# Attention 1, dense blocks: the sources' features as the stationary operand, the clipped counts moving as 256 columns

## The chip, the cores and the metric

The kernel runs on one core of a Trainium2 chip. The metric is the device time of one launch in microseconds (us). Before the change three runs took 5505.89, 5550.96 and 5581.69 us, so the median is 5550.96 us. Engines are named as in the profile: PE (matmuls), PEld (weight loads of PE), DVE (vector), ACT (scalar), POOL (GpSimd) and SP (queue of DMAs). Each has its own list of instructions, whose order is fixed when the program is built, and waits for the others through semaphores.

## The reference

A graph with 6250 nodes and 200000 edges, sorted by destination, passes two layers of attention and then a layer that makes messages from edge attributes. The change touches only the first attention layer (4 heads of 16 features):

```python
feat = (x @ W).reshape(num_nodes, H, D)
el = jnp.sum(feat * attn_l[None], axis=-1)
er = jnp.sum(feat * attn_r[None], axis=-1)
e = jax.nn.leaky_relu(el[src] + er[dst], NEG_SLOPE)
m = jax.ops.segment_max(e, dst, num_segments=num_nodes)
ee = jnp.exp(e - m[dst])
s = jax.ops.segment_sum(ee, dst, num_segments=num_nodes)
alpha = ee / s[dst]
msg = feat[src] * alpha[:, :, None]
rst = jax.ops.segment_sum(msg, dst, num_segments=num_nodes)
return rst + bias.reshape(1, H, D)
```

Each destination node gets a weighted mean of its sources' features, one weight for each edge and head. The weight is exp(leaky_relu(el + er)), which is a product of a source's factor and a destination's factor, and only which of two such products is used depends on the sign of el + er.

## The kernel before

The nodes lie in 49 blocks of 128. In attention 1 the first 31 blocks of destinations ("gather blocks") are computed edge by edge. For each block POOL issues 34 indirect DMAs (L319), each fetching 128 rows of `table1` into a tile `G`, of which there are six buffers of eight fetches. DVE and PE make one-hot matrices and weights (`attend`, L353 to L377: `ohr`, `pe`, `w`, `msg`, `halves`, and the scatter matmul at L377).

The last 18 blocks ("dense blocks", DENSE1 = 18) are computed in 9 pairs by `dense1`, L845 to L940. For these, the kernel first builds a matrix of edge counts for each block of destinations: `count`, L758 to L785, compares indices on DVE (L767), multiplies one-hots on PE (L778), copies on ACT (`ca`, L780) and writes `counts` to DRAM from ACT's queue (L782). A pair then goes over all 49 source blocks in 7 chunks of 7 (HS = 7), and in each chunk over the 4 heads: 9 x 7 x 4 = 252 steps. In one step

- ACT makes a step function `ramp` of el + er, 7 times 128 x 256 (L885),
- DVE takes the minimum of it and of the counts, giving the clipped counts `up`, 128 x 1792 (L887),
- PE adds up (`add`, L891 to L906): for each of the 7 source blocks and each of the 2 destination blocks one weight load of 128 columns of `up` and one matmul in which 102 columns of `rc` move (L905). `rc` holds, for each source, its features times each of the two factors, split into three bf16 parts: 4 heads x 2 factors x 17 x 3 = 408 columns and 2 ones. The result stands with destinations on the partitions, in two PSUM banks `up0` and `up1`, one for each destination block.

Once for each chunk, PE also adds all counts without clipping into `every` (L899): there the features, 103 columns of `rc`, are stationary, and 256 columns of counts move. At the end of a pair (`end`, L910 to L938) ACT copies `every` (L913), PE turns it with 4 transposes (L917), and DVE sums the three parts from the turned tile (L922, twice) and directly from the PSUM of `up0` and `up1` (L926, four times), then subtracts, multiplies by the destination's factors and adds (L929 to L937), and `finish1` makes the rows of the next layer's tables.

`rhs1`, the DRAM copy of `rc`, is filled once by `fill_rhs1` (L682 to L700) in seven pieces during gather blocks 1 and 2.

The three kinds of work are interleaved in the program: after each group of gathers some steps of counting and of `dense1` follow, by due counts. `step` runs a PE part one step after what feeds it. The order within each engine's list is then settled by the framework's scheduler, so lines of neighbouring steps stand mixed there.

The names needed below: `bank()` and `small()` take from one ring of two PSUM banks (`small`), shared by the counting, the transposes and `finish1`. Attention 2 follows after the last end; it doesn't change.

Of the kernel before, what the change touches and what calls it, by code (L numbers as in the profile page):

```python
# [30 lines left out]
F32 = mybir.dt.float32  # L31
# [5 lines left out]
OP = mybir.AluOpType  # L37
AX = mybir.AxisListType
# [4 lines left out]
P = 128  # L43
# [8 lines left out]
HS = 7  # L52
# [14 lines left out]
def gnn_kernel(ctx: ExitStack, tc: tile.TileContext, x, src, dst, attr4, attr8,  # L67
               W1, al1, ar1, b1, W2, al2, ar2, b2,
               Wl0, Wl1, Ws0, Ws1, Wm1, Wm2, Wtp, Wf0, Wf1, src_t, dst_t, attr4_t, attr8_t, out):
    nc = tc.nc  # L70
    N, D = x.shape
    E = src.shape[0]
    NB = -(-N // P)
    FULL = N // P
    REST = N - FULL * P
    HD = W1.shape[1]
    H1, DH = al1.shape
# [38 lines left out]
    def bank():  # L116
        return ps_bank.tile([P, 512], F32, tag="small" if ps_bank is ps_sm else "bank", name="bank")
# [5 lines left out]
    ident = const.tile([P, P], F32, name="ident")  # L123
# [35 lines left out]
    fin = one.enter_context(tc.tile_pool(name="fin1", bufs=1))  # L159
# [8 lines left out]
    for name, v in (("di", dst), ("si", src)):  # L168
        t = find.tile([GP, ROWT + WCAP], I32, name=name)
# [505 lines left out]
    NG = NB - DENSE1  # L675
    dn = one.enter_context(tc.tile_pool(name="dn", bufs=2))
    C1 = 3 * (DH + 1)
    W1R = 2 * H1 * C1 + 2
    rhs1 = dram.tile([P, NB, W1R], BF16, name="rhs1")
    deg1 = pool.tile([P, DENSE1], F32, name="deg1")  # L680

    def fill_rhs1(b0, n):  # L682
        t = dn.tile([P, HS, R1], F32, name="t1c", bufs=1)
        nc.sync.dma_start(t[:, :n], rows_of(table1, b0, n))
        x = dn.tile([P, HS, 2, H1, DH + 1], F32, name="x1", bufs=1)
        for j in range(2):
            ex = t[:, :n, HD + (1 + j) * H1:HD + (2 + j) * H1]
            nc.vector.tensor_tensor(x[:, :n, j, :, :DH], t[:, :n, :HD].rearrange("p b (h d) -> p b h d", h=H1),
                                    ex[:, :, :, None].to_broadcast([P, n, H1, DH]), op=OP.mult)
            nc.vector.tensor_copy(x[:, :n, j, :, DH:], ex[:, :, :, None])  # L690
        r = dn.tile([P, HS, W1R], BF16, name="rc")
        nc.vector.memset(r[:, :, 2 * H1 * C1:], 1.0)
        for j in range(2):
            rj = r[:, :, j * H1 * C1:(j + 1) * H1 * C1].rearrange("p b (f s) -> p b f s", s=3)
            xj = x[:, :n, j].rearrange("p b h d -> p b (h d)")
            nc.scalar.copy(rj[..., 0], xj)
            nc.vector.tensor_tensor(xj, xj, rj[..., 0], op=OP.subtract)
            nc.scalar.copy(rj[..., 1], xj)
            nc.vector.tensor_tensor(rj[..., 2], xj, rj[..., 1], op=OP.subtract)
        nc.sync.dma_start(rhs1[:, b0:b0 + n], r)  # L700

    cut = one.enter_context(tc.tile_pool(name="cut", bufs=1))
# [142 lines left out]
    def dense1():  # L845
# [14 lines left out]
        for b0 in range(NG, NB, 2):  # L860
            n = min(2, NB - b0)
            ahead = load(b0, n, 0)
            erb = dn.tile([P, H1, 2 * P], F32, name="erb", bufs=1)
            for h in range(0, H1, 2):
                pe = bank()
                for j in range(2):
                    for k in range(n):
                        c = j * 2 * P + k * P
                        nc.tensor.matmul(pe[:, c:c + P], er1[:, b0 + k, h + j:h + j + 1].to_broadcast([P, P]), ident,
                                         start=True, stop=True)  # L870
                nc.scalar.copy(erb[:, h:h + 2, :n * P], pe.rearrange("p (j c) -> p j c", j=2)[:, :, :n * P])

            sums = {}
            yield []
            for h0 in range(0, NB, HS):
                ct, r = ahead
                if h0 + HS < NB:
                    ahead = load(b0, n, h0 + HS)
                by_head = r[:, :, :2 * H1 * C1].rearrange("p b (j h f) -> p b j h f", j=2, h=H1)
                for h in range(H1):  # L880
                    ramp = dn.tile([P, HS, 2 * P], BF16, name="ramp1")
                    up = pool.tile([P, LONG], BF16, tag="row", name="up1", bufs=2)[:, :HS * 2 * P].rearrange(
                        "p (h a) -> p h a", h=HS)
                    for i in range(HS):
                        nc.scalar.activation(ramp[:, i, :n * P], erb[:, h, :n * P], AF.Relu,  # L885
                                             bias=sel1[:, h0 + i, h:h + 1], scale=STEEP)
                    nc.vector.tensor_tensor(up[:, :, :n * P].rearrange("p h (a d) -> p h a d", d=QN),  # L887
                                            ramp[:, :, :n * P].rearrange("p h (a d) -> p h a d", d=QN),
                                            ct[:, :n].rearrange("p k a h d -> p h (k a) d"), op=OP.min)

                    def add(h0=h0, h=h, r=r, ct=ct, up=up, by_head=by_head, b0=b0, n=n, sums=sums):  # L891
                        if h0 + h == 0:
                            sums["ups"] = [ps_dn.tile([P, 512], F32, tag=f"up{k}", name=f"up{k}")[:, :2 * H1 * C1].rearrange(
                                "p (h j f) -> p h j f", h=H1, j=2) for k in range(n)]
                            sums["every"] = ps_dn.tile([P, 2, 2 * P], F32, tag="every", name="every")
                        ups, every = sums["ups"], sums["every"]
                        for i in range(HS if h == 0 else 0):
                            for j in range(2):
                                nc.tensor.matmul(every[:HH + 1, j, :n * P].rearrange("p (k d) -> p k d", d=QN),  # L899
                                                 r[:, i, (2 + j) * HH:(3 + j) * HH + 1],  # L900
                                                 ct[:, :n, :, i, :].rearrange("p k a d -> p (k a) d"),
                                                 start=h0 + i + j == 0, stop=h0 + i + j == NB)
                        for i in range(HS):
                            for k in range(n):
                                nc.tensor.matmul(ups[k][:, h], up[:, i, k * P:(k + 1) * P], by_head[:, i, :, h, :],  # L905
                                                 start=h0 + i + h == 0, stop=h0 + i + h == NB + H1 - 2)  # L906

                    yield [add]

            def end(b0=b0, n=n, sums=sums):  # L910
                ups, every = sums["ups"], sums["every"]
                whole = dn.tile([HH + 1, 2, 2 * P], F32, name="whole", bufs=1)
                nc.scalar.copy(whole[:, :, :n * P], every[:HH + 1, :, :n * P])  # L913
                turned = bank().rearrange("p (k j c) -> p k j c", k=2, j=2)
                for k in range(n):
                    for j in range(2):
                        nc.tensor.transpose(turned[:, k, j, :HH + 1], whole[:, j, k * P:(k + 1) * P],  # L917
                                            ident[:HH + 1, :HH + 1])
                s2 = dn.tile([P, 2, H1, DH + 1], F32, name="s2", bufs=1)
                v = dn.tile([P, 2, 2, H1, DH + 1], F32, name="v1", bufs=1)  # L920
                for k in range(n):
                    nc.vector.tensor_reduce(s2[:, k].rearrange("p (j h) d -> p j (h d)", j=2),  # L922
                                            turned[:, k, :, :HH].rearrange("p j (f s) -> p j f s", s=3),
                                            axis=AX.X, op=OP.add)
                    for j in range(2):
                        nc.vector.tensor_reduce(v[:, k, j], ups[k][:, :, j].rearrange("p h (d s) -> p h d s", s=3),  # L926
                                                axis=AX.X, op=OP.add)
                nc.vector.tensor_copy(deg1[:, b0 - NG:b0 - NG + n, None], turned[:, :n, 1, HH:HH + 1])
                nc.vector.tensor_tensor(v[:, :n, 1], s2[:, :n], v[:, :n, 1], op=OP.subtract)  # L929
                for j in range(2):  # L930
                    nc.vector.tensor_tensor(v[:, :n, j], v[:, :n, j],
                                            pq[:, b0:b0 + n, j * H1:(j + 1) * H1, None].to_broadcast([P, n, H1, DH + 1]),
                                            op=OP.mult)
                total = fin.tile([P, 2, HD + H1], F32, name="sumsd")
                nc.vector.tensor_add(total[:, :n, :HD].rearrange("p k (h d) -> p k h d", h=H1), v[:, :n, 0, :, :DH],
                                     v[:, :n, 1, :, :DH])
                nc.vector.tensor_add(total[:, :n, HD:, None], v[:, :n, 0, :, DH:], v[:, :n, 1, :, DH:])  # L937
                finish1(b0, n, total[:, :n, :])  # L938

            yield [end]  # L940
# [549 lines left out]
```

## Time and profile before

| what | value | from |
|---|---|---|
| median of three runs | 5550.96 us | times |
| the profiled execution | 5588.02 us, span 5586.3 us | times, page |
| mean granted clock of PE | 0.720 | page |
| PE, DVE, ACT, POOL busy over the span | 61%, 63%, 52%, 47% | page, part 1 |
| weight loads of L905 | 272.9 us busy, x3528, 131 ns mean | page, part 5 |
| `up` on DVE (L887) | 273.8 us, x252, 1087 ns mean | page, part 5 |
| L905 first and last start | 510.4 and 2403.7 us | rows of this line |

The profiled execution is one launch, 37 us above the median. Steps of `dense1` run from about 500 to 2400 us after the span's start, beside the gathers and the counting; attention 2 lies at about 2420 to 3000 us, the message layer after it. In a line of groups the name of the tile written stands before the arrow, the tiles read after it; then come the number of instructions, the busy time in us, the mean in ns, and behind the second bar the idle time just before them with what ended most of it. A busy time counts overlapped instructions of one engine once, so it is smaller than the number times the mean.

### The profile page before, as it was taken

What the parts mean: (1) busy time and instruction counts of PE and PEld (TensorE: products, weight loads), DVE (VectorE), ACT (ScalarE), POOL (GpSimd) and SP (SyncE); (2) the same over time, 40 slices, a digit from 0 to 9 for tenths busy, and PEclk for the clock granted to TensorE, in tenths of its full rate; (3) what the DMA queues carried; (4) which work ended last, traced back from release to release, by engine and by line L of the source; (5) the groups of instructions that cost most, each with busy time, mean ns of one, the idle gap of its engine ahead of it and who ended that gap; (6) DMA issues with size and microseconds to landing.
All of it is one profiled execution on the core that took longest, in us unless ns stands there. A gap on an engine that the chain in (4) does not pass through costs nothing. (4 is left out here: it accounts for less than half of the span.)

```text
span 5586.3 us, 66809 instructions
## 1 busy us (share of the span) xinstructions
PE 3395.3 (61%) x22075; PEld 2519.0 (45%) x22076; DVE 3498.1 (63%) x5531; ACT 2900.8 (52%) x6921; POOL 2639.6 (47%) x2684
## 2 busy tenths in 40 slices
PE   3124554644555545569995566676667666677676
PEld 2124444544444445558884334344434344444444
DVE  4255555655656655668885566666666666666667
ACT  2024655754655656669995344444444444444444
POOL 2655545545345445310003555555556556555553
PEclk9998555655666556669997676767767666767667
DMA  4243433433334434454442111111111111111111
GB/s 105 60 125 98 120 109 110 137 104 108 110 113 118 118 101 118 115 188 151 163 165 70 45 48 47 46 49 48 48 47 49 46 48 49 48 47 49 47 48 30
DMA packets 348033, 480.97 MB, mean 86 GB/s; under 512 B 190602, under 2 KB 236208, under 8 KB 343695
## 3 DMA queue, kind: packets, MB, share of 16 engines
q1 hardware_dynamic: 199014, 238.86, 14.2%
q0 software_dynamic: 85776, 147.31, 11.2%
q10 hardware_dynamic: 62872, 90.28, 4.6%
q8 instruction: 181, 2.97, 0.2%
q14 instruction: 190, 1.55, 0.1%
HBM read 367.21 MB, written 108.97 MB: 85 GB/s over the span
## 5 line engine op out<-in xcount | busy, mean ns | idle before, releaser
L319 POOL DMA_INDIRECT G<-table,srcc x1563 | 1475.4, 944 | 1556.8 <-issue 676.6
L319 POOL DMA_INDIRECT G<-table,srcw x1054 | 1091.9, 1036 | 987.3 <-DVE w L362 384.4
L1300 PE MATMUL whole<-halves,ohr 128*128 128x512 f32 x1563 | 798.7, 647 | 24.3 <-issue 23.3
L885 ACT ACTIVATE ramp<-erb,sel 128x256 bf16<-128x256 f32 x1764 | 756.5, 499 | 1.9 <-DVE up L887 1.6
L1252 ACT ACTIVATE hid<-big 128x512 f32<-128x512 f32 x392 | 233.9, 597 | 951.5 <-PE big L1250 419.5
L780 ACT CAST ca<-small 128x392 bf16<-128x392 f32 x784 | 350.2, 482 | 644.3 <-remote 413.0
L778 PE MATMUL small<-key,lo 128*128 128x98 bf16 x3136 | 339.0, 260 | 484.3 <-ACT ca L780 213.3
L1300 PEld LDWEIGHTS whole<-halves,ohr 128*128 128x128 f32 x1563 | 418.1, 283 | 438.2 <-issue 373.7
L1250 PE MATMUL big<-a8t,wm_sb 16*128 16x512 f32 x392 | 294.5, 840 | 394.8 <-issue 346.6
L1274 ACT ACTIVATE g<-G,a 128x128 f32<-128x128 f32 x1563 | 506.9, 401 | 11.2 <-DMA G<-table,srcc 9.6
L1181 ACT ACTIVATE ramp<-erb,sel 128x256 bf16<-128x256 f32 (+1 forms) x1225 | 491.8, 499 | 23.5 <-DVE up L1185 16.8
L778 PEld LDWEIGHTS <-lo 128*128 128x128 bf16 x3136 | 262.4, 128 | 533.5 <-issue 523.0
L767 DVE TENSOR_TENSOR lo<-slots,turned 128x2048 bf16<-128x2048 bf16 x196 | 239.5, 1222 | 418.5 <-remote 206.0
L1293 DVE TENSOR_TENSOR halves<-mess,halves 128x1024 fp32r<-128x1024 f32 x196 | 239.1, 1220 | 350.6 <-ACT halves L1287 201.2
L1250 PE MATMUL big<-hid,wm_sb 128*128 128x512 f32 x392 | 356.7, 1011 | 112.4 <-ACT hid L1252 99.0
L905 PE MATMUL up<-rc,up 128*128 128x102 bf16 x3528 | 323.5, 268 | 144.8 <-DVE up L887 106.4
L1258 PE MATMUL big<-wtp_sb,hid 64*128 64x128 f32 x3126 | 289.4, 331 | 142.6 <-issue 79.0
L1258 PEld LDWEIGHTS big<-wtp_sb,hid 64*128 64x128 f32 x3126 | 244.2, 229 | 246.9 <-issue 140.0
L377 PE MATMUL whole<-halves,ohr 128*128 128x136 f32 x1054 | 248.1, 388 | 173.1 <-issue 80.0
L905 PEld LDWEIGHTS <-up 128*128 128x128 bf16 x3528 | 272.9, 131 | 176.5 <-DVE up L887 127.3
L887 DVE TENSOR_TENSOR up<-ramp,ctc 128x1792 bf16<-128x1792 bf16 x252 | 273.8, 1087 | 97.2 <-ACT ramp L885 64.2
L377 PEld LDWEIGHTS whole<-halves,ohr 128*128 128x128 f32 x1054 | 218.3, 294 | 185.2 <-issue 84.5
(294 smaller groups left out, 6252.9 us busy)
## 6 DMA issues: line engine op xcount, KB each, us to landing
counts<-ca ACTq DMA_DIRECT2D x196, 392.0 KB
ct<-counts SPq DMA_DIRECT2D x192, 392.0 KB
rc<-rhs SPq DMA_DIRECT2D x63, 717.5 KB
oht<-dlow SPq DMA_DIRECT2D x31, 1088.0 KB
ctc<-counts SPq DMA_DIRECT2D x504, 56.0 KB
G<-table,srcc POOLq DMA_INDIRECT x1563
G<-table,srcw POOLq DMA_INDIRECT x1054
a8t<-attr_rows SPq DMA_DIRECT2D x391, 16.0 KB
```

Of the source, the lines that this page charges most:

```text
L319: nc.gpsimd.indirect_dma_start(out=G[:, c, :], out_offset=None, in_=table, in_offset=bass.IndirectOffsetOnAxis(ap=idx[:, c:c + 1], axis=0))
L377: nc.tensor.matmul(acc, oh[:, c, :], ms[:, c].rearrange("e s f -> e (s f)"), start=start and c == 0, stop=stop and c == n - 1)
L778: nc.tensor.matmul(ps[:, k * NKEY:(k + 1) * NKEY], lo[:, a, :, r], ky[:, a, :, r], start=True, stop=True)
L780: nc.scalar.copy(ca[:, :, i * W:(i + WBANK) * W].rearrange("p h (k d) -> p h k d", d=W), ps[:, :WBANK * NKEY].rearrange("p (k h d) -> p h ...
L885: nc.scalar.activation(ramp[:, i, :n * P], erb[:, h, :n * P], AF.Relu, bias=sel1[:, h0 + i, h:h + 1], scale=STEEP)
L887: nc.vector.tensor_tensor(up[:, :, :n * P].rearrange("p h (a d) -> p h a d", d=QN), ramp[:, :, :n * P].rearrange("p h (a d) -> p h a d", d ...
L905: nc.tensor.matmul(ups[k][:, h], up[:, i, k * P:(k + 1) * P], by_head[:, i, :, h, :], start=h0 + i + h == 0, stop=h0 + i + h == NB + H1 - 2)
L1181: nc.scalar.activation(ramp[:, h, :n * P], erb[:, :n * P], AF.Relu, bias=sel2[:, h0 + h, :], scale=STEEP)
L1250: nc.tensor.matmul(ph, w, (hid[-1] if j else x)[:, :npr * P], start=True, stop=True)
L1258: nc.tensor.matmul(pw[:, c, :], hid[1][half, j * P:(j + 1) * P], wtp_sb[half].rearrange("x p u -> x (p u)"), start=True, stop=True)
L1274: nc.scalar.activation(g0[:, c], G[:, c, :], AF.Copy, scale=a0[:, c, :])
L1300: nc.tensor.matmul(acc, oh[:, c, :], ms[:, c].rearrange("e s h i u -> e (s h i u)"), start=start, stop=stop)
```

## The change

Stationary and moving operand of the clipped sums change places, as they already stand for `every`. For each source block and head there is now one weight load of 102 columns of `rc` and one matmul in which both blocks' `up`, 256 columns, move. The sums stand with features on the partitions, so the end of a pair copies them from PSUM (`some`, two copies on ACT), turns them with 8 transposes on PE into two more banks of the ring, and sums the parts from there. So that the 102 columns of one head are contiguous, and that `every` still has two runs of 103, `rc` is laid out by pairs of heads (205 columns: 102 of one head, a one, 102 of the next, with the two factors in swapped order), and the operations of `fill_rhs1` and of the end are split by head of the pair.

```diff
-    W1R = 2 * H1 * C1 + 2
+    HW = 4 * C1 + 1
+    W1R = H1 // 2 * HW
...
-        x = dn.tile([P, HS, 2, H1, DH + 1], F32, name="x1", bufs=1)
+        x = dn.tile([P, HS, H1 // 2, 2, 2, DH + 1], F32, name="x1", bufs=1)
         for j in range(2):
-            ex = t[:, :n, HD + (1 + j) * H1:HD + (2 + j) * H1]
-            nc.vector.tensor_tensor(x[:, :n, j, :, :DH], t[:, :n, :HD].rearrange("p b (h d) -> p b h d", h=H1),
-                                    ex[:, :, :, None].to_broadcast([P, n, H1, DH]), op=OP.mult)
-            nc.vector.tensor_copy(x[:, :n, j, :, DH:], ex[:, :, :, None])
+            ex = t[:, :n, HD + (1 + j) * H1:HD + (2 + j) * H1].rearrange("p b (q h) -> p b q h", h=2)
+            for h in range(2):
+                xh = x[:, :n, :, h, j if h == 0 else 1 - j]
+                nc.vector.tensor_tensor(
+                    xh[..., :DH], t[:, :n, :HD].rearrange("p b (q h d) -> p b q h d", h=2, d=DH)[:, :, :, h],
+                    ex[:, :, :, h, None].to_broadcast([P, n, H1 // 2, DH]), op=OP.mult)
+                nc.vector.tensor_copy(xh[..., DH:], ex[:, :, :, h, None])
...
                         if h0 + h == 0:
-                            sums["ups"] = [ps_dn.tile([P, 512], F32, tag=f"up{k}", name=f"up{k}")[:, :2 * H1 * C1].rearrange(
-                                "p (h j f) -> p h j f", h=H1, j=2) for k in range(n)]
+                            sums["ups"] = [ps_dn.tile([P, 2, 2 * P], F32, tag=f"up{k}", name=f"up{k}")
+                                           for k in range(H1 // 2)]
...
+                        q, h = divmod(h, 2)
                         for i in range(HS):
-                            for k in range(n):
-                                nc.tensor.matmul(ups[k][:, h], up[:, i, k * P:(k + 1) * P], by_head[:, i, :, h, :],
-                                                 start=h0 + i + h == 0, stop=h0 + i + h == NB + H1 - 2)
+                            c = q * HW + h * (2 * C1 + 1)
+                            nc.tensor.matmul(ups[q][:2 * C1, h, :n * P], r[:, i, c:c + 2 * C1], up[:, i, :n * P],
+                                             start=h0 + i + h == 0, stop=h0 + i + h == NB)
...
+                some = dn.tile([2 * C1, H1 // 2, 2, 2 * P], F32, name="some", bufs=1)
+                for q in range(H1 // 2):
+                    nc.scalar.copy(some[:, q, :, :n * P], ups[q][:2 * C1, :, :n * P])
...
+                for h in range(2):
+                    c = h * (C1 + 1)
+                    nc.vector.tensor_reduce(s2[:, :n, :, h], turned[:, :n, :, c:c + C1].rearrange(
+                        "p k j (f s) -> p k j f s", s=3), axis=AX.X, op=OP.add)
...
                 for k in range(n):
-                    nc.vector.tensor_reduce(s2[:, k].rearrange("p (j h) d -> p j (h d)", j=2),
-                                            turned[:, k, :, :HH].rearrange("p j (f s) -> p j f s", s=3),
+                    turned = bank().rearrange("p (h c) -> p h c", h=H1)
+                    for h in range(H1):
+                        nc.tensor.transpose(turned[:, h, :2 * C1], some[:, h // 2, h % 2, k * P:(k + 1) * P],
+                                            ident[:2 * C1, :2 * C1])
+                    nc.vector.tensor_reduce(v[:, k].rearrange("p q h j d -> p (q h) (j d)"),
+                                            turned[:, :, :2 * C1].rearrange("p h (f s) -> p h f s", s=3),
                                             axis=AX.X, op=OP.add)
-                    for j in range(2):
-                        nc.vector.tensor_reduce(v[:, k, j], ups[k][:, :, j].rearrange("p h (d s) -> p h d s", s=3),
-                                                axis=AX.X, op=OP.add)
...
-                nc.vector.tensor_tensor(v[:, :n, 1], s2[:, :n], v[:, :n, 1], op=OP.subtract)
-                for j in range(2):
-                    nc.vector.tensor_tensor(v[:, :n, j], v[:, :n, j],
-                                            pq[:, b0:b0 + n, j * H1:(j + 1) * H1, None].to_broadcast([P, n, H1, DH + 1]),
-                                            op=OP.mult)
+                for h in range(2):
+                    vh = [v[:, :n, :, h, j if h == 0 else 1 - j] for j in range(2)]
+                    nc.vector.tensor_tensor(vh[1], s2[:, :n, :, h], vh[1], op=OP.subtract)
                     for j in range(2):
+                        f = pq[:, b0:b0 + n, j * H1:(j + 1) * H1].rearrange("p b (q h) -> p b q h", h=2)[:, :, :, h, None]
+                        nc.vector.tensor_tensor(vh[j], vh[j], f.to_broadcast([P, n, H1 // 2, DH + 1]), op=OP.mult)
...
```

The two additions that make `sumsd` (L935 and L937) are likewise split in two, one for each head of the pair.

## The prediction

> **What bounds the kernel now.** I read the groups of the page first, to see what the touched lines cost, then the engines by stretch, then the list of waits, then the order in time.
>
> ```profile
> L319 POOL DMA_INDIRECT G<-table,srcw x1054 | 1091.9, 1036 | 987.3 <-DVE w L362 384.4
> ...
> L885 ACT ACTIVATE ramp<-erb,sel 128x256 bf16<-128x256 f32 x1764 | 756.5, 499 | 1.9 <-DVE up L887 1.6
> ...
> L905 PE MATMUL up<-rc,up 128*128 128x102 bf16 x3528 | 323.5, 268 | 144.8 <-DVE up L887 106.4
> ```
>
> The line to be changed is the last: 323.5 us of PE, in 252 groups of 14. Before it PE waited 106.4 us for `up` from DVE. In the same steps ACT's ramp takes 756.5 us, so in a dense step alone ACT has 3.0 us, PE 1.28 us and DVE 1.09 us of work.
>
> ```profile
> 560.00:2400.00 1840.00, 995.64 (x9040) 891.18 (x9040) 1081.16 (x1910) 1101.36 (x2699) 863.13 (x825) 0.60 0.40 113
> 2520.00:2940.00 420.00, 384.13 (x4065) 346.92 (x4063) 360.07 (x648) 420.00 (x1077) 0.00 (x0) 1.00 0.47 160
> ```
>
> Columns: stretch, length, busy us of PE, PEld, DVE, ACT, POOL, granted clock, DMA share, GB/s. In the stage of the change (first row) no engine is full: PE 54%, DVE 59%, ACT 60%, POOL 47%. In attention 2 (second row) ACT is full. So the first stage isn't set by an engine but by engines waiting for each other in turn:
>
> ```profile
> POOL G L319 <- DVE w L362: 359.7, 37, 40.4
> ...
> DVE lo L767 <- PE small L778: 165.7, 89, 14.1
> ACT ca L780 <- PE small L778: 143.1, 110, 16.3
> ...
> PE up L905 <- DVE up L887: 104.7, 80, 4.5
> ```
>
> These are totals over the same 1840 us (us, times, longest). POOL's fetches stand still for 547 us in all until DVE gives a buffer of `G` back (359.7 for L362, 117.1 for L367, 71 for smaller lines), and 79.5 us more for a fetch of the next run; with them 627 of 1840 us, 34%. In the rest POOL issues, about 1.25 us for each fetch (945 ns and 0.30 idle), and DVE, ACT and PE stand still when they need a fetch that isn't there. So a delay of DVE counts in full in about a third of the stage, and in the rest is partly covered by fetches that run anyway. I take one half, with a third and all as bounds, for what a delay in the middle of the stage is worth. Nobody waits long for L905 itself: its own releases are 12.4 us (ACT), 6.0 and 1.4 us (DVE). It counts by what stands behind it on PE, L778 above all.
>
> **The clipped sums on PE.** Removed: 3528 loads and 3528 matmuls of 102 columns. Added: 1764 of each, with 256 columns. The new form isn't in the trace, but `every` (L899) is nearly it: 103 stationary columns of `rc`, 256 columns moving, bf16.
>
> ```profile
> 794.55 3.20 PE L899 MATMUL every<-ctc,rc 128*103 128x256 bf16 x14
> ...
> 1555.50 1.37 PE L905 MATMUL up<-rc,up 128*128 128x102 bf16 x14
> ...
> 1578.61 1.69 PE L899 MATMUL every<-ctc,rc 128*103 128x256 bf16 x14
> ...
> 1667.88 0.82 PE L905 MATMUL up<-rc,up 128*128 128x102 bf16 x14
> ```
>
> Rows of PE in order of time: start, length, line, count. Each line has a slow and a fast form. 14 old matmuls take 1.37 or 0.82 us; less one matmul's own length (283 and 206 ns) that is 84 or 47 ns from start to start. 14 of `every` take 3.20 or 1.69 us, less 421 and 270 ns: 213 or 109 ns. One new matmul replaces two old ones: 213 for 168, or 109 for 94. For a step of 7: +0.31 us slow, +0.10 us fast. The mean old group is 323.5/252 = 1.28 us, which is 84% slow and 16% fast, so +0.28 us a step and **+70 us** of PE over 252 steps. Halving the count of instructions gains nothing, because the old ones were already paced by their columns (204 for two) and the new ones are by 256. Bounds: a third to all of it, 23 to 70 us; I take half, **+35 us**.
>
> A weight load of 128 columns of `up` takes 144 ns at the median, one of 103 of `rc` 207 ns; 3528 against 1764 is 508 against 365 us. Both lie under matmuls that are spaced by their columns, so I count no gain; if loads did set the pace it would be -143 us, which only rival C uses. The Trainium skill (TensorE: Matmul & The Clock Gate, section Weight-path perf modes) says that fast weight load works only with 128 weights that aren't fp32, so the 102 columns lose it. That speaks against the change, and by it each load would be up to twice an old one, no gain from half the number; the rows give 1.4 times.
>
> The same page (section What's actually happening) says that PE's clock opens only after about 3.4 us of sustained work. The trace has 0.60 in this stage and 1.00 in attention 2. By that rule groups of 1.70 us for 1.37 us would open it a little more often; I found no way to size it and put nothing in the sum.
>
> **The end of a pair, 9 times.** In the rows of one end the sums stand like this:
>
> ```profile
> 1572.48 1.20 DVE L926 TENSOR_REDUCE v<-up 128x68 f32<-128x204 f32 x4 [1.07 <-remote]
> ...
> 1574.66 0.90 PE L917 MATMUL bank<-ident,whole 103*128 103x103 f32 x4
> ```
>
> DVE reads `up` at once, and only `every` goes over ACT and PE. After the change everything does. ACT: two copies of 102x512, each like L913 (586 ns), +1.2 us. PE: 8 transposes of 102 columns; four of L917 take 0.90 us, so +1.8 us. DVE: four sums at 360 ns go, two of twice that size come; L1198, 390 elements, takes 556 ns, so about 575 ns each: 1.44 against 1.15. Subtract, multiply and add are split by head, 5 operations become 10; the smallest there is 160 ns and the old ones 280 to 290 ns, so some 0.6 us more. DVE together +0.3 us. The copies and transposes are links of one chain, overlapping in part, then a sum: about 2.5 us later for the results at each end, 22 us over 9. DVE's list in the built program has the two new sums directly behind those of `every`, and `msg`, `halves` and the next `w` behind them: whoever waits for these gives `G` back to POOL. PE has the transposes ahead of L377 and `every`, ACT has the second copy, which waits for the last add, ahead of `halves`; and the two extra banks come out of the ring of two that the counting uses. Bounds: 0 (all under gathers) to 5 us an end, 45 us; I take **+22 us**. SP and POOL get no new instruction, and no DMA changes its size.
>
> **fill_rhs1, 7 times.** Each of 14 multiplications (615 ns for 448) becomes two of 224; with 283 ns for 128 each is about 385 ns, +0.15. Each of 14 small copies (182 ns) becomes two, +0.15. Together +4 us on DVE; ACT's casts keep their number and size. Bounds 0 to 8 (strides), I take **+4 us**.
>
> **Sum.** 35 + 22 + 4 = +61 us. On the profiled execution's 5588 us that is 5649; that execution lay 37 us above the median, and the terms are absolute, so from the median it is 5551 + 61 = **5612 us**, +1.1%. Lowest and highest by the bounds: +23 and +123.
>
> **Rivals.** A verdict needs 2%, 111 us, which is also about what a measurement of this kernel can tell from no change (the three runs spread over 76 us).
>
> B, slower by over 2%: the turn at the pair's end becomes a stop of the whole ring. DVE stands at the new sums until ACT has copied and PE has turned; behind it stand the lines that free `G`, POOL stops, and its fetches are then missing. One such stop of POOL lasts 359.7/37 = 9.7 us now. Nine of 10 us are 90 us, with the 39 above 129: 5680 us. If PE's 70 us count in full too: 5715. It decides from 8 us an end ((111 - 39)/9). For: in the row above, waits for PE inside an end are already there, and the longest are 40 us. Against: the sums of `every` already made this detour at the same place, and DVE waited only a few us in all there (2.8 for L360, 0.8 for L917).
>
> C, faster by over 2%: the built program keeps nearly all of the order elsewhere but moves gathers' lines around each end on DVE and PE. If that, or PE's shorter list, takes away a third of POOL's 359.7 us, that is -120; with the loads setting PE's pace (-143, by half -72) in place of +35, and the other 26 kept, -166: 5385 us. The order alone, -120 + 61, gives 5492 and no verdict; between the two the case begins at 5440. For: these waits are of one line, long and few. Against: nothing in the rows shows loads setting the pace, and a moved line can as well make a wait longer.
>
> D, that it doesn't do what it says: the built program has 1764 loads and matmuls for 3528 each, so this is out, except that the moving 256 columns might cost other than `every`'s.
>
> **How the numbers follow.** The forecast, a small loss or nothing that can be told, 0.46. B 0.36: its point is 8 us an end, and small delays in a ring of waiting engines tend to grow. C 0.18. The range goes from the upper part of C, 5440, to B with all of PE, 5720; the forecast's own is 5560 to 5660. Faster 0.18, same 0.46, slower 0.36.
>
> **What would show it.** In the changed profile: matmuls of the clipped sums x1764 with about 213 or 109 ns from start to start and a group of 7 at 1.7 or 0.9 us, PE busy there about 390 us in place of 323.5; loads x1764 at about 200 ns; two copies of about 590 ns and 8 transposes at each end; the stage from 500 to 2400 us longer by some 60 us and attention 2 and the message layer unchanged. POOL's waits for DVE in that stage above 650 us speak for B, below 430 for C. A mean clock far from 0.60 there, or `up` matmuls that start closer than 213 ns at the slow clock, would make the prediction wrong.

## The result, and the profile after

The changed kernel takes 5541.78 us (median of 20 runs, 5523.15 to 5577.78), the kernel before, run beside it, 5548.45 us (20 runs, 5494.07 to 5581.69). The ratio on record, which isn't simply that of the two medians (0.9988), is 1.0003, with a 95% interval of 0.9981 to 1.0025: no difference, where +1.1% was forecast. One plain fact is needed to read what follows: launches of either kernel took about 5550 us in some of the comparisons and about 4431 us in others, alike within one comparison and both on the same chip (two of the chips gave both), so every ratio below is to the kernel before in the same comparison, and "at 5550" or "at 4431" says which kind it was.

The groups of the changed kernel's profile (span 5563.5 us, before 5586.3):

```profile
L319 POOL DMA_INDIRECT G<-table,srcw x1054 | 1084.7, 1029 | 915.1 <-DVE w L362 373.5
...
L892 ACT ACTIVATE ramp<-erb,sel 128x256 bf16<-128x256 f32 x1764 | 756.7, 499 | 4.4 <-DVE up L894 2.1
...
L785 PE MATMUL small<-key,lo 128*128 128x98 bf16 x3136 | 323.2, 253 | 376.3 <-issue 182.1
...
L913 PE MATMUL up<-up,rc 128*102 128x256 bf16 x1764 | 364.8, 371 | 133.2 <-DVE up L894 101.9
...
L913 PEld LDWEIGHTS <-rc 128*102 128x102 bf16 x1764 | 302.4, 179 | 149.4 <-issue 142.3
...
L377 PE MATMUL whole<-halves,ohr 128*128 128x136 f32 x1054 | 234.0, 373 | 158.0 <-DVE halves L332 89.8
```

The count is halved, as the diff says, and PE's own line grew, but from 323.5 to 364.8 us, by 41 and not by 70. The counting's matmuls (L785, before L778), whose code is the same, fell from 339.0 to 323.2 us, and those of L377 from 248.1 to 234.0. So most of the 41 us came back on other lines of PE, whose single matmuls got shorter (L785 253 ns in the mean for 260, L377 373 for 388). The same stretches as before show it too:

```profile
560.00:2400.00 1840.00, 1006.80 (x7397) 913.81 (x7397) 1081.81 (x1932) 1109.99 (x2717) 854.94 (x825) 0.63 0.40 113
2520.00:2940.00 420.00, 384.07 (x4070) 347.03 (x4070) 361.51 (x654) 420.00 (x1077) 0.00 (x0) 1.00 0.48 162
```

In the stage of the change the granted clock is 0.63 for 0.60, and PE's busy time 1006.8 for 995.6 us. The stage itself did not lengthen: `up` matmuls start from 522.9 to 2400.5 us, before from 510.4 to 2403.7. Attention 2 is as it was. The waits of that stretch (total us, times, longest):

```profile
POOL G L319 <- DVE w L362: 349.1, 29, 48.4
...
ACT ca L787 <- remote: 294.6, 57, 32.1
...
DVE lo L774 <- PE small L785: 191.4, 96, 14.0
...
POOL G L319 <- DVE msg L367: 152.3, 17, 42.2
...
DVE lo L774 <- remote: 131.8, 14, 25.8
```

The waits of POOL's fetches of `G` for DVE make 552 us for 547, in the middle between the marks set for B (650) and C (430): neither came. Two rows end in "remote", that is, the profile found no instruction whose end released the engine. They were there before as well, larger than any row that the prediction showed but one, and it read past them:

```profile
ACT ca L780 <- remote: 348.3, 84, 15.4
...
DVE lo L767 <- remote: 196.4, 25, 26.6
```

The parts of the change look as costed. PE in order of time, start, length, count, two groups of 7:

```profile
1407.64 1.70 PE L913 MATMUL up<-up,rc 128*102 128x256 bf16 x7
...
1461.41 0.93 PE L913 MATMUL up<-up,rc 128*102 128x256 bf16 x7
```

1.7 or 0.9 us, the two forms that were read off `every`. And one end of a pair:

```profile
922.91 0.59 ACT L929 COPY some<-up 102x512 f32<-102x512 f32 x1 [1.33 <-PE up L913]
...
924.81 0.89 PE L940 MATMUL bank<-ident,some 102*128 102x102 f32 x4
...
925.73 0.58 DVE L942 TENSOR_REDUCE v<-bank 128x136 f32<-128x408 f32 x1
...
926.28 0.89 PE L940 MATMUL bank<-ident,some 102*128 102x102 f32 x4
...
927.21 0.58 DVE L942 TENSOR_REDUCE v<-bank 128x136 f32<-128x408 f32 x1 [0.63 <-PE bank L940]
```

Copies, transposes and sums have the lengths of the prediction (590, 900 for four, 575 ns), and DVE stands 0.63 us at the second sum here; over all 18 such sums it waits 5.5 us for the transposes.

### The profile page after: what moved, and what is told of

It is laid out like the page before. It is cut to its first block, busy times and chain, and to the rows that moved or that the text cites. A ratio compares the mean times of both kernels' runs of the same rounds, so it can differ in the third digit from the quotient of the medians.

```text
span 5563.5 us, 63519 instructions
## 1 busy us (share of the span) xinstructions
PE 3408.7 (61%) x20383; PEld 2536.5 (46%) x20384; DVE 3504.3 (63%) x5586; ACT 2909.2 (52%) x6939; POOL 2630.0 (47%) x2684
## 3 DMA queue, kind: packets, MB, share of 16 engines
q0 software_dynamic: 85776, 147.31, 11.2%
## 5 line engine op out<-in xcount | busy, mean ns | idle before, releaser
L785 PE MATMUL small<-key,lo 128*128 128x98 bf16 x3136 | 323.2, 253 | 376.3 <-issue 182.1
L1200 ACT ACTIVATE ramp<-erb,sel 128x256 bf16<-128x256 f32 (+1 forms) x1225 | 491.6, 496 | 22.7 <-DVE up L1204 17.8
L785 PEld LDWEIGHTS <-lo 128*128 128x128 bf16 x3136 | 257.5, 124 | 417.0 <-issue 401.7
L913 PE MATMUL up<-up,rc 128*102 128x256 bf16 x1764 | 364.8, 371 | 133.2 <-DVE up L894 101.9
L913 PEld LDWEIGHTS <-rc 128*102 128x102 bf16 x1764 | 302.4, 179 | 149.4 <-issue 142.3
L377 PE MATMUL whole<-halves,ohr 128*128 128x136 f32 x1054 | 234.0, 373 | 158.0 <-DVE halves L332 89.8
L377 PEld LDWEIGHTS whole<-halves,ohr 128*128 128x128 f32 x1054 | 204.5, 278 | 179.0 <-DVE halves L332 94.6
```

The source lines that it names most:

```text
L377: nc.tensor.matmul(acc, oh[:, c, :], ms[:, c].rearrange("e s f -> e (s f)"), start=start and c == 0, stop=stop and c == n - 1)
L785: nc.tensor.matmul(ps[:, k * NKEY:(k + 1) * NKEY], lo[:, a, :, r], ky[:, a, :, r], start=True, stop=True)
L913: nc.tensor.matmul(ups[q][:2 * C1, h, :n * P], r[:, i, c:c + 2 * C1], up[:, i, :n * P], start=h0 + i + h == 0, stop=h0 + i + h == NB)
L1200: nc.scalar.activation(ramp[:, h, :n * P], erb[:, :n * P], AF.Relu, bias=sel2[:, h0 + h, :], scale=STEEP)
```

## The experiments

The expectations name theories by number or letter. Theories 1 and B: PE and the ends have slack, so that next to nothing counts on any launch. Theory 2: PE's time counts by about half, as forecast, and something else gave it back. Theory A: the forecast's cost is real, and at 5550 the waits without a releaser cover it. Theory C, not the rival C of the prediction: the turn is dear, the matmuls are a gain, and the two cancel. Where they speak of a slower and a faster chip, read 5550 and 4431.

### First comparison, at 4431: doses of PE work

A dose is the same work in another amount. **e1_pe_twice** puts a second matmul, with zeros stationary, behind each of the 1764; **e2_pe_3_more** does so for 3 of the 7 source blocks only.

```diff
+                            if i < 7:      # e2: 3
+                                nc.tensor.matmul(ups[q][:2 * C1, h, :n * P], none, up[:, i, :n * P],
+                                                 start=False, stop=h0 + i + h == NB)
```

> The changed kernel with a second matmul behind each of the 1764 of the clipped sums: same 256 columns moving, same PSUM, a stationary tile of zeros, so it adds nothing to the result and about 1764 x 213 ns = 376 us at the slow clock, 192 us at the fast one, to PE. Theory 1 (PE has slack in this stage: the ring of fetches and DVE sets the pace and PE's work lies beside it): less than +40 us on the kernel before. Theory 2 (as in the prediction: PE's time counts by about half, and the change's cost was given back by something else, order or clock): +100 to +190 us.

> The same with the second matmul for only 3 of every 7 source blocks: 756 more matmuls, +82 to +161 us of PE. Theory 1: within 15 us of the kernel before, and less than 3/7 of what the full doubling costs (a threshold). Theory 2: +40 to +80 us, 3/7 of the doubling (proportional).

Measured: 1.0105 (1.0089 to 1.0120), 4478.06 us, and 1.0092 (1.0078 to 1.0106), 4473.22 us, the kernel before taking 4431.27.

**e3_pe_seventh** goes the other way: one source block of each seven is added.

```diff
-                        for i in range(HS):
+                        for i in range(1):
```

> The changed kernel with only the first source block of each chunk of seven added into the clipped sums (left out: six sevenths of these sums, so the attention of the dense blocks is not the reference's). PE loses 1512 of 1764 matmuls and loads, about 310 us of busy time. Theory 1: 0 to -20 us. Theory 2: -100 to -160 us.

Measured: 1.0037 (1.0023 to 1.0051), 4447.08 us.

**e4_end_twice** copies, turns and sums twice at each end.

```diff
-                for q in range(H1 // 2):
+                for q in (*range(H1 // 2), *range(H1 // 2)):
...
-                for k in range(n):
+                for k in (*range(n), *range(n)):
```

> The changed kernel with the new part of each pair's end done twice: the two copies of the sums, the eight transposes and the two sums of parts. Theory 1 (the end's extra time goes under fetches that run anyway): within 15 us of the kernel before. Theory 2 (each end pays what it is delayed by): 9 ends x 2.5 to 5 us = +22 to +45 us. If the ring stops as in the rival that ends slower: +90 us.

Measured: 1.0096 (1.0081 to 1.0112), 4470.52 us.

All four lie above 1. Read against the kernel before, as the expectations do, e1 (+46 us) and e3 (+16 us) fit neither theory, since a part of the loss is in all four. Between themselves they can be read at once: e1 is 0.68% above e3, 30 us, and its PE is busy 228.6 us more (lines below), so 13% of that PE time shows in the time, give or take 4%. What the changed kernel itself does at 4431 came only with h1 below.

### Second and third comparisons, at 5550: each part alone

**a1_after** is the changed kernel again, **b1_before** a single launch of the kernel before. **a3_no_turn** drops the copies, transposes and their banks, and makes the sums from the tile that is there already:

```diff
-                for q in range(H1 // 2):
-                    nc.scalar.copy(some[:, q, :, :n * P], ups[q][:2 * C1, :, :n * P])
...
-                    for h in range(H1):
-                        nc.tensor.transpose(turned[:, h, :2 * C1], some[:, h // 2, h % 2, k * P:(k + 1) * P],
-                                            ident[:2 * C1, :2 * C1])
```

**b2_turn_only** is the kernel before with only the new end: copies of `up0` and `up1`, 8 transposes, two sums for four.

```diff
+                for k in range(n):
+                    nc.scalar.copy(some[:, k, :2 * H1 * C1], ups[k][:2 * C1].rearrange("p h j f -> p (h j f)"))
...
-                    for j in range(2):
-                        nc.vector.tensor_reduce(v[:, k, j], ups[k][:, :, j].rearrange("p h (d s) -> p h d s", s=3),
-                                                axis=AX.X, op=OP.add)
```

> The changed kernel itself, on the chip of this call. Its first comparison was on a chip where the kernel before takes 5548 us; the first experiments ran on one where it takes 4431 us, and there all four variants of the changed kernel were 0.4 to 1.05% above the kernel before. Theory A (the change costs what was worked out, or half of it, and on the first chip the waits with no releaser in the trace cover it): +0.6 to +1.0% where the kernel before takes about 4430 us, 0 where it takes about 5550 us. Theory B (PE and the end have slack on any chip, and the variants' own edits cost what they showed): within 0.3% on either.

> The first part of the change alone: the matmuls with 256 columns moving and the new layout stay, but the end of a pair neither copies the clipped sums nor turns them; DVE sums parts of the turned tile of all counts in their place (left out: the clipped sums never reach the result; the shares' denominators are held above 1 so that numbers stay finite). Theory A with the end as the cost: equal to the kernel before within 0.2%. Theory A with PE's columns as the cost: as the changed kernel, +0.5 to +1.0% on the faster chip. Theory B: within 0.3%.

> The second part alone: the kernel before with its 3528 matmuls of 102 columns, and at each pair's end two copies by ACT, eight transposes by PE and two sums of 408 elements by DVE in place of the four sums from PSUM (left out: the clipped sums are turned as if they stood by features, so the dense blocks' result is not the reference's; denominators held above 1). Theory A with the end as the cost: as the changed kernel, +0.5 to +1.0% on the faster chip. With PE's columns as the cost: within 0.2%. Theory B: within 0.3%.

> The kernel before, for its profile on the chip of this call: theory A expects next to no waits without a releaser in the stage of the dense blocks where the time is about 4430 us, and ACT and DVE busy for about 80% there; theory B says nothing of it.

Measured, the kernel before at 5577.1 us: a1 0.9999 (0.9977 to 1.0022), a3 0.9950 (0.9926 to 0.9975), b2 1.0041 (1.0015 to 1.0068); b1 5559.48 us. That looked like theory C: the matmuls a gain of 0.5%, the turn a loss of 0.4 to 0.5%. So both were run again, beside **f1_turn_later**, where the end is two steps, ACT's copies in the first and the rest in the next:

```diff
+                sums["copied"] = whole, some
+
+            yield [end]
+
+            def turn(b0=b0, n=n, sums=sums):
...
-    n_dense = -(-DENSE1 // 2) * (2 + H1 * (NB // HS))
+    n_dense = -(-DENSE1 // 2) * (3 + H1 * (NB // HS))
```

> The changed kernel again. Theory C, formed on the last call (two effects that cancel: with half as many instructions on PE the clipped sums gain about 0.5%, the end of a pair loses about 0.4%): 1.000 where the kernel before takes about 5550 us. Theory B (slack, the parts' differences were their own order of instructions): the same. On the faster chip, if the gain of the sums comes from PE's late events alone, it is missing there and the loss stays: +0.4 to +0.8%.

> The matmuls with 256 columns and the new layout alone, without copies and turn at the end, as before (the clipped sums never reach the result; denominators held above 1). Theory C: 0.995 again on a chip where the kernel before takes about 5550 us; on the faster chip, where PE's events are not late, 1.000 to 1.004. Theory B: 1.000 within 0.2% on either.

> The kernel before with the copies, transposes and sums of the new end alone, as before (its dense blocks' result is not the reference's; denominators held above 1). Theory C: 1.004 again on the slower chip, and +0.4 to +0.7% on the faster one, since the chain ACT, PE, DVE is there on any chip. Theory B: 1.000 within 0.2%.

> The changed kernel with its end in two steps: the three copies of ACT in one, the transposes, DVE's sums and the rest one step later, so that PE and DVE come to the turned sums when the copies are long done. Theory C: the loss of the end goes and the gain of the sums stays, 0.995 of the kernel before on the slower chip, faster than both. Theory B: as the changed kernel, 1.000.

Measured, the kernel before at 5549.69 us: c1 0.9980 (0.9957 to 1.0003), c3 0.9991 (0.9967 to 1.0016), c2 1.0007 (0.9980 to 1.0033), f1 0.9985 (0.9966 to 1.0003). Neither part repeated. The same pair of kernels moved by 0.3 to 0.4% between two comparisons, more than one interval holds, so parts below about 0.4% cannot be told here, and moving the turn gained nothing over the changed kernel. The traces do part the two where the clock is concerned: in the stretch from 560 to 2400 us it is 0.63 and 0.64 with the new matmuls alone (a3, c3), as in the changed kernel, and 0.61 and 0.60 with the turn alone (b2, c2), as in the kernel before.

### Fourth comparison, at 5550: the doses

The edits of e1 and e4 once more, with the changed kernel beside them.

> The changed kernel, as the base of the two others. Where the kernel before takes about 5550 us: 0.998 to 1.002. Where it takes about 4430 us: theory A (the worked-out cost is real, and only the late waits cover it) 1.005 to 1.010; theory B (slack on any chip) 0.998 to 1.002.

> The changed kernel with a second matmul (stationary zeros, the same 256 columns) behind each of the clipped sums: nine times the PE time that the change added. On the slower chip: theory B and A both within 0.3% of the changed kernel, if the waits cover PE; if PE's time is paid by half and was given back by something else, +2 to +3%. On the faster chip: 1.0105 of the kernel before, as measured; the difference from the changed kernel is then the price of 365 us of PE.

> The changed kernel with the copies, transposes and sums of the new end done twice. On the slower chip: within 0.3% of the changed kernel if ends go under other waits, +0.4% if each end pays about 2.5 us. On the faster chip: 1.0096 of the kernel before, as measured; under theory A the changed kernel is then about half of that above 1, under theory B at 1.000.

Measured, the kernel before at 5569.98 us: g1 0.9995 (0.9973 to 1.0017), g2 1.0077 (1.0053 to 1.0102), g3 1.0021 (0.9997 to 1.0044). The page's groups of g2, and the stage in g1 and then in g2:

```profile
L915 PE MATMUL up<-up,rc 128*102 128x256 bf16 x1764 | 523.4, 325 | 138.3 <-DVE up L896 98.9
...
L918 PE MATMUL up<-up,none 128*102 128x256 bf16 x1764 | 523.6, 326 | 10.3 <-issue 9.6
```

```profile
560.00:2400.00 1840.00, 995.57 (x7394) 902.69 (x7393) 1079.31 (x1930) 1105.37 (x2713) 851.80 (x826) 0.64 0.40 113
560.00:2400.00 1840.00, 1088.63 (x8822) 997.95 (x8821) 1052.85 (x1887) 1061.66 (x2602) 862.39 (x831) 0.74 0.39 111
```

The two lines overlap each other, so together they are busy some 524 us: twice the matmuls for 364.8 us once is +44%, not +100%, with the clock at 0.74. Over the whole span PE's busy time goes from 3394.7 (g1) to 3516.2 us, +121.5. The time goes up by 0.82% of 5570, 46 us: 38% of what PE was really given, give or take 15%. Theories A and B had both expected less than 0.3% here, so both missed.

### Fifth and sixth comparisons, at 4431: the changed kernel, and without its turn

**h1_after** is the changed kernel, **k1_no_turn** the edit of a3, **k2_before** a single launch of the kernel before.

> The changed kernel once more, for the chip it falls on. Where the kernel before takes about 4430 us: 1.005 to 1.010 if the change's cost is real and only the late waits of the slower chip cover it; 0.998 to 1.002 if PE and the ends have slack on any chip. Where it takes about 5550 us: 0.998 to 1.002, as in all comparisons so far.

> The matmuls with 256 columns and the new layout alone, no copies and no turn at the end (the clipped sums never reach the result; denominators held above 1). Where the kernel before takes about 4430 us: 1.000 to 1.002 if the turn is the cost, 1.005 to 1.008 if it is the matmuls, the layout or the order of instructions that they bring. Where it takes about 5550 us: 0.995 to 1.000, as twice before.

> The kernel before, for its profile beside the last run. Where it takes about 4430 us: ACT and DVE busy for about 80% of 500 to 1700 us, next to no waits without a releaser; the stage of the dense blocks ends some 25 to 35 us earlier than in the changed kernel if the cost lies there, and the filling of the operands near 250 to 350 us some 4 us earlier.

Measured: h1 1.0080 (1.0065 to 1.0096), 4464.11 us for 4430.4; k1 1.0030 (1.0017 to 1.0043), 4442.86 us for 4432.59; k2 4435.64 us. So at 4431 there is a loss, about 35 us, in the range that theory A gave, and 22 us of it (uncertain by 9) go with the turn. With h1 the first four can be read; the two comparisons' medians of the kernel before lie within 1 us. The line of engine totals of each page, for k2, h1, e1, e2 and e3:

```profile
PE 3130.2 (71%) x22075; PEld 2356.0 (53%) x22076; DVE 3480.2 (78%) x5531; ACT 2920.3 (66%) x6921; POOL 2668.8 (60%) x2684
```

```profile
PE 3129.0 (70%) x20383; PEld 2369.9 (53%) x20384; DVE 3487.3 (78%) x5586; ACT 2925.9 (66%) x6939; POOL 2665.3 (60%) x2684
```

```profile
PE 3213.2 (72%) x22147; PEld 2468.5 (55%) x22148; DVE 3491.6 (78%) x5587; ACT 2926.3 (65%) x6939; POOL 2655.7 (59%) x2684
```

```profile
PE 3166.5 (71%) x21139; PEld 2403.2 (54%) x21140; DVE 3489.7 (78%) x5587; ACT 2928.3 (65%) x6939; POOL 2663.1 (60%) x2684
```

```profile
PE 2984.6 (67%) x18871; PEld 2192.7 (49%) x18872; DVE 3487.7 (78%) x5586; ACT 2930.5 (66%) x6939; POOL 2658.2 (60%) x2684
```

The change leaves PE's total at 3129.0 for 3130.2 us: nothing was added. The stretch from 500 to 1800 us, for k2, e3, h1, e2 and e1 (the number after the five engines is the granted clock):

```profile
500.00:1800.00 1300.00, 892.40 (x8699) 815.00 (x8699) 1037.76 (x1857) 1044.00 (x2585) 882.84 (x824) 0.66 0.54 155
500.00:1800.00 1300.00, 764.71 (x5700) 663.51 (x5700) 1032.64 (x1870) 1046.36 (x2584) 884.54 (x829) 0.59 0.54 154
500.00:1800.00 1300.00, 887.40 (x7010) 814.01 (x7009) 1024.65 (x1858) 1034.84 (x2557) 891.43 (x830) 0.72 0.54 153
500.00:1800.00 1300.00, 908.36 (x7617) 840.65 (x7617) 1016.91 (x1844) 1025.32 (x2531) 886.69 (x830) 0.79 0.53 152
500.00:1800.00 1300.00, 961.14 (x8463) 897.87 (x8462) 1014.53 (x1836) 1015.90 (x2514) 876.34 (x827) 0.84 0.53 152
```

The doses give one price:

| against h1 | PE busy | time | share | clock, 500 to 1800 us |
|---|---|---|---|---|
| e3, a seventh | -144.4 us | -0.43%, -19 us | 13% | 0.59 |
| h1, the changed kernel | 0 | 0 | | 0.72 |
| e2, 3 of 7 twice | +37.5 us (3166.5) | +0.12%, +5 us | 14% | 0.79 |
| e1, all twice | +84.2 us | +0.25%, +11 us | 13% | 0.84 |

Each difference of two ratios is uncertain by about 0.2%, so the single shares are rough, e2's above all, and all three stand against the same h1; e1 against e3, above, gives 13% without it. The clock follows the dose, and the counting's matmuls, whose code is the same in all, show it: they take 261, 243, 234 and 224 ns in the mean in e3, h1, e2 and e1 (250 in k2).

The ends: from the last matmul of a pair's clipped sums to its last `sumsd`, k2 takes 60.4 us over the nine ends, h1 83.1, k1 74.5, e4 98.3. The change adds 22.7 us, 2.5 us an end, of which k1, which has neither copies nor turn of the clipped sums, already has 14.1. At 5550 two traces of the kernel before give 88.6 and 93.2 us, four of the changed one 119.5 to 132.3, some 34 us more. e4 adds 15.2 us to h1's and costs 0.16%, 7 us. In g3 the ends grow from g1's 119.5 to 164.7 us and the time by 0.26%, 14 us. Neither cost is clear of its uncertainty (0.2 and 0.3%).

One thing in h1 nobody had forecast. The first indirect DMAs of POOL, k2 and then h1:

```profile
110.14 0.96 POOL L319 DMA_INDIRECT G<-table,srcw  x1 [62.19 <-DVE wseg_i L627]
```

```profile
109.81 0.96 POOL L716 DMA_INDIRECT wpart_i<-in_dst,wseg_i  x1 [62.15 <-DVE wseg_i L627]
...
128.25 0.94 POOL L716 DMA_INDIRECT wpart_i<-in_dst,wseg_i  x1 [0.34 <-PE pe L360]
129.50 0.94 POOL L319 DMA_INDIRECT G<-table,srcw  x1 [0.30 <-issue]
```

In the changed kernel the scheduler put all ten fetches of a search (L716, before L709) ahead of the first fetch of `G`, which comes 19 us later. The traces of a3, c3 and k1, which have the split of `fill_rhs1` but no turn, keep the old order; those of b2 and c2, which have the turn but not the split, have the new one, as do e1 to e4. So the edit at a pair's end brought it, the four doses share it with h1, and each run without the turn is also one without the new start. In h1 the fetches of `G` lie 19 us behind k2's at first, 9 to 11 us through the blocks up to the first pair's end at 584 us, and 30 us behind at the last. At 5550 a part stays too: the 150th fetch is issued at 373.2 to 374.5 us in the four traces with the old order, and at 379.7 to 381.0 in the nine with the new one.

## Why the prediction was wrong, step by step

**The clipped sums on PE, +70 us of PE time: this is the term that failed.** Its working per matmul held: 213 or 109 ns for 168 or 94, groups of 1.7 or 0.9 us. What failed is "84% slow" carried over to the new form (364.8 us over 252 groups is 1.45 us a group, by the same reckoning 67% slow), and "I found no way to size it and put nothing in the sum" for the clock. At 5550 the line itself grew by 41 us, other lines of PE shrank, and PE's whole busy time rose from a mean of 3391.7 us (two traces of the kernel before) to 3397.6 (four of the changed one, 3388.0 to 3408.7), which isn't clear of the scatter; at 4431 it did not rise at all. The runs show the cause as far as a dose can: with a seventh, all, 3 of 7 twice and all twice of this work, the granted clock of the stage is 0.59, 0.72, 0.79 and 0.84, for 0.66 in the kernel before. At 5550 the new matmuls alone raise it as the whole change does, and the turn alone does not. Added work of PE opens its clock, and the clock pays most of it back on the lines around. The Trainium skill (TensorE: Matmul & The Clock Gate, section What's actually happening) says that the clock has two settings only, half and full, chosen by how busy PE was in the last 3.4 us or so; the spacings of 213 and 109 ns agree with two settings, and the mean clock that rises with the dose agrees with the rest. The rule that spoke for a gain here was cited and given no number; this was the mistake. The sign set for it, a clock far from 0.60, was too coarse: 0.63 for 0.60 on some 1000 us of busy PE is, as an estimate, up to 50 us.

**Exposure, one half.** For PE time that is really there the doses give about 38% at 5550, near the lower bound of a third, and 13% at 4431. POOL's share of waiting, 34%, came close to the first, but by luck as much as by reason: at 4431 the exposure is under half of it. Times 6 us of real PE time, the term is 2 us, not 35.

**The end of a pair, +22 us.** The delay came out near the forecast at 4431, 22.7 us over nine ends in h1, but partly by luck: copies and turn, which were to make nearly all of it, go with 8.6 us, and 14.1 are in k1 as well; at 5550 it is some 34 us. As a cost in time it was probably too high: the doubled ends cost 14 us of 45 at 5550 and 7 us of 15 at 4431, a third to a half, which would make some 11 us of the 34 and 10 of the 22.7, but neither cost is clear of its uncertainty. The prediction had bounded it by 0 and 45 and took the delay itself.

**fill_rhs1, +4 us.** DVE's whole busy time is 3504.3 us for 3498.1, which fits in size with the 0.3 us an end; its cost was not measured alone. The start order above was forecast for no term; it came with the turn.

**B.** The turn does not stop the ring. Over the 18 sums DVE waits 5.5 us, the fetches' waits for DVE stayed at 552 us, and doubling the turn cost 0.26%. B's point was 8 us an end; in time it is a little over 1 by the doubled ends. **C**, faster by over 2%, needed either POOL's waits to shrink or loads that set PE's pace, and neither is seen. Of the theory C of the experiments: the parts alone, averaged over two comparisons, are -0.30% (without the turn) and +0.24% (turn only), which sum to what was measured, but each pair of values differs by 0.3 to 0.4%, and at 4431 the part without the turn has the other sign. It is not shown. **The loads** (302.4 us for 272.9, mean 179 ns for 131) stayed under the matmuls: from start to start most of L913 stands at 213 or 109 ns, and none below 107. The skill's rule on fast weight load (same page, section Weight-path perf modes) fits the slower load of 102 columns, and it did not matter here.

**The sum by measured prices** at 5550 is 2 + 11 = 13 us, 0.2%, plus at most a few for `fill_rhs1` and for the start order. The four comparisons of the changed kernel gave 1.0003, 0.9999, 0.9980 and 0.9995. What is left of the difference is within the scatter between comparisons and has no explanation here.

**At 4431** the changed kernel loses 35 us. Read from the traces, some 11 us may be the start order and some 10 us the turn, which come and go together; the other 13 are in k1 as well, which has PE's new matmuls, DVE's split and no turn. By the dose they cannot be PE's time, which is unchanged. Whether they come from DVE's split or from lines that moved is open. The start order was not undone by itself, so how the 22 us divide is argued, not shown.

**The waits without a name.** The "remote" waits are the other thing that the prediction missed. One of them in the kernel before, engines in order of time:

```profile
940.07 2.04 PE L869 MATMUL bank<-ident,er 128*128 128x128 f32 x8 [5.44 <-remote]
...
959.22 0.59 ACT L871 COPY erb<-bank 128x512 f32<-128x512 f32 x1 [18.50 <-remote]
...
959.85 0.48 PE L778 MATMUL small<-key,lo 128*128 128x98 bf16 x4 [17.74 <-ACT erb L871]
```

PE's last matmul of L869 ends at 942.11, and ACT, which waits for nothing else that the rows show, starts 17.1 us later. In between DVE, ACT and PE all stand, and only POOL issues fetches. Counted over the trace, 532 of the 2284 events of PE's semaphore come more than 0.5 us after the end of the last matmul before them, 1642 us in sum; in the changed kernel 469, 1487 us; in k2 5 of 2458, 26 us. The stage of 1894 us at 5550 takes 1419 us at 4431 (415.5 to 1834.8), while attention 2, which has no fetches, takes 561 us in both, from its first `ramp` to its last. PE, DVE and ACT all stand in 359 of the 1840 us from 560 to 2400 in the kernel before, and in 9 of the 1300 us from 500 to 1800 in k2. So the stage that the prediction called "engines waiting for each other in turn" stands to a good part still for late events, and its terms could not be sized by the waits that have a name alone. That the late events cover the change's cost at 5550, as theory A had it, is not shown: added PE time counted there more, not less, than at 4431. Why the change loses 35 us at 4431 and none at 5550 stays open.

## What to carry to other kernels

Price an added piece of work by a dose, more and less of the same, and read the engine's total busy time with it: a line that grows under a gated clock can leave the total where it was. In a list of waits, look first at those that have no releaser and at gaps in which all engines stand; while they are large, a share of waiting read from the named rows is no measure of exposure. Look also at the first hundred microseconds of a rebuilt program, since an edit in one place can turn an early order on a queue: here one at the end of each pair moved the first fetches by 19 us.

## What was unexpected of the hardware

- Events of PE's semaphore came up to 29 us after the last matmul, in the comparisons at 5550, and nearly only while POOL issues indirect DMAs: in the kernel before 206 (663 us) in its stretch from 480 to 2420 us, one (6.5 us) in attention 2, and 300 (793 us) after it. At 4431 k2 has 5 (26 us). The packets of the fetches' queue take as long in both (11.2% of 16 engines' 5586.3 us, 14.0% of 4433.9). What makes them late is open.
- The clock of PE is a reserve: with twice the matmuls of one line (1764 more), the busy time of the line and its double is 44% above the changed kernel's, and the stage's clock rose from 0.64 (g1) to 0.74.
- A load of 102 columns takes 205 ns at the median, one of 128 columns 144 ns, and cost nothing that could be seen below 256 moving columns.
